# Transposing the row maxima in the bank of the next source, behind the values in even units, with a split low part and earlier statistics

## The chip, the cores and the metric

The kernel runs on one core of a Trainium2 chip. The metric is the device time of one execution in microseconds (us); lower is better. A core has a matmul engine (TensorE, PE in the profile, with its weight loads as PEld), a vector engine (VectorE, DVE), an activation engine (ScalarE, ACT), a general engine (GpSimd, POOL) and a queue engine that issues DMAs (SyncE, SP). Matmul results are written to PSUM, in banks of 128 partitions x 512 float32; VectorE and ScalarE read them there, GpSimd does not read PSUM in this kernel.

## The reference

One transformer block: self-attention with modulation, cross-attention on a context, and an MLP, for 16 samples of 256 tokens with width 256, 16 heads of width 16 and an MLP of 1024, in float32.

```python
x_norm = modulate(_ln(x), shift_a, scale_a)
q, k, v = jnp.split(x_norm @ W_qkv + b_qkv, 3, axis=-1)
attn_w = softmax(einsum('bhqd,bhkd->bhqk', q, k) * scale)
x = x + gate_a * (attn(attn_w, v) @ W_proj + b_proj)
q_c = _ln(x) @ W_qc + b_qc
k_c, v_c = jnp.split(_ln(context) @ W_kvc + b_kvc, 2, axis=-1)
x = x + cross_attn(q_c, k_c, v_c) @ W_cproj + b_cproj
x_norm2 = modulate(_ln(x), shift_m, scale_m)
x = x + gate_m * (gelu(x_norm2 @ W_mlp1 + b_mlp1) @ W_mlp2 + b_mlp2)
```

## The kernel before

**Units and beats.** The attention work is cut into 32 units, numbered from 0: a unit is the self-attention (s) or the cross-attention (c) of one sample. The order is s0 to s4, then s5, c0, s6, c1 and so on to s15, c10, then c11 to c15. So from unit 5 to unit 26 the odd units are s and the even ones c; from 26 on all are c. Each unit has eight beats, `beat(n, k)` with k from 0 to 7, and the code of a beat is the order in which each engine is given its work: PE, ACT, DVE, POOL and SP all keep program order, so an instruction that waits holds up everything behind it on its engine. After the units comes the MLP, which the change does not touch.

**What a beat holds.** A beat of unit n works on several units at once. `visit(n, k)` multiplies score rows of unit n + 1 into the bank pair s, whose row maxima VectorE then takes (TENSOR_REDUCE, mx<-s), and the transposed scores of unit n into the bank pair st. `exps()` then has ScalarE make the exponentials (pt<-st). Even beats add `av_part`, 16 matmuls of exponentials by values into a bank o (128*32 tiles). Odd beats add `lanes`, 24 projection matmuls in two interleaved chains for the queries, keys and values of units n + 2 and n + 3 and the output projection of an earlier unit. `cur`, `prev` and `nxt` are units n, n - 1 and n + 1; `q2`, `q3`, `q4` are units n + 2, n + 3, n + 4; `lc` is q4 and `lx` is q3 where they are cross-attentions, `ls` is q4 where it is a self-attention; `p1`, `p2`, `p3` are what follows the attention of units n - 1, n - 2, n - 3.

**Preparing a unit.** For unit n + 3 the layernorm has three steps: bn_stats (`steps[0]`), bn_aggr on VectorE with the power on GpSimd (`steps[1]`: mv, rs) and the normalised rows xn on GpSimd (`steps[2]`). TensorE transposes xn into a bank psT (`T.turn`, half f = 0 in beat 0 and f = 1 in beat 2 where the source is `ready`, both in beat 2 where not); ScalarE makes the high part of the result (`xTh`) and VectorE or GpSimd the low part (`xTl`), so that three matmuls of rounded numbers stand for one in float32. In the same way `to_stack` makes of the projected queries and keys a high part on ScalarE (`h_qc`, `h_k`) and a low part (`l_qc`, `l_k`): for each of two halves, f = 0 and 1, one VectorE instruction that reads the bank ps and subtracts the high part. DMAs on SP's queue carry both into the stack `big`, from which scores are multiplied.

**The maxima.** `m_part(u, half)` turns the maxima of half of a unit's heads: a transpose on TensorE (`psm`), a multiplication by -1 on ScalarE (`m`) and a DMA on SP into row 63 of the unit's queries, so that scores come out with the maximum subtracted. It stands in beat 0 (second half of unit n) and in beat 4 (first half of unit n + 1).

**Banks.** psm, psT and o come from two buffers in turn (`SHORT`), the projections from two others (`LONG`). A bank taken anew waits for the last reader of what it held: ps_k of beat 5 takes the bank of ps_qc, so it waits for the last reader of ps_qc; ps_qc of beat 1 takes that of ps_k or ps_kc. Sums of the exponentials come with o, are copied out by ScalarE (`oT`), fetched by a DMA as S (`pull`) and inverted (`recip`) in beat 2 of even units and beat 3 of odd ones.

Of the kernel before, what the change touches and what calls it, by code (L numbers as in the profile page):

```python
# [16 lines left out]
P = 128  # L17
# [4 lines left out]
def pixart_block(  # L22
# [45 lines left out]
    def ps_gen(name, tag=None):  # L68


        if tag is None and ps_turn[0] is not None:
            ps_turn[0] ^= 1
            tag = (SHORT, LONG)[ps_turn[0]]
        tag = tag or SHORT
        return psum.tile([P, 512], F32, tag=tag, name=name, bufs=2)
# [368 lines left out]
    def to_stack(W, src, bias, dst, which, name):  # L444

        o = Box()
        lo_row = (2, 1)[which]

        o.W, o.src, o.tok, o.name = W, src, False, name

        def first():
            o.ps = ps_gen(f"ps_{name}", LONG)
            mm3(o.ps[:, 0:N], W, 0, src.xT)

        def third():
            mm3(o.ps[:, N:], W, 1, src.xT)

        def second():  # L460
            third()
            high()

        def high():
            o.hi = work.tile([P, KC, N], F32R, tag="qkh", name=f"h_{name}", bufs=3)
            for f in range(KC):
                ACT.activation(o.hi[:, f], o.ps[:, f * N:(f + 1) * N], AF.Identity, bias=bias[f])

        def low():
            o.lo = work.tile([P, KC, N], F32R, tag="qkl", name=f"l_{name}", bufs=3)  # L470
            for f in range(KC):
                DVE.scalar_tensor_tensor(o.lo[:, f], o.ps[:, f * N:(f + 1) * N], bias[f], o.hi[:, f],
                                         ALU.add, ALU.subtract)

        def low_pool():
            o.lo = work.tile([P, KC, N], F32R, tag="qkl", name=f"l_{name}", bufs=3)
            y = work.tile([P, KC, N], F32, tag="y", name=f"y_{name}", bufs=1)
            for f in range(KC):
                ACT.activation(y[:, f], o.ps[:, f * N:(f + 1) * N], AF.Identity, bias=bias[f])
            POOL.tensor_tensor(o.lo, y, o.hi, ALU.subtract)  # L480

        def send(part, q=SP):

            row = (0, 3 - lo_row, lo_row)[part]
            q.dma_start(dst[row:row + 4 * 31 + 1:4].bitcast(F32), (o.hi if part < 2 else o.lo).bitcast(F32))

        o.send = send
        o.parts = [first, second, low]
        o.third = third
        o.low_pool = low_pool  # L490
        o.high, o.low = high, low
        o.send_high = lambda: [send(part) for part in range(2)]
        o.send_low = lambda: send(2)
        o.steps = [first, second]
        return o
# [169 lines left out]
                              AX.X, ALU.max)  # L665
        yield

    def m_part(u, hf):

        pst = ps_gen(f"psm_{u.n}_{hf}", SHORT)  # L670
        PE.transpose(pst[:16, :P], u.mx[:, hf].rearrange("p r a t -> p (r a t)"), ident)
        m = work.tile([16, P], F32R, tag="m", name=f"m_{u.n}_{hf}", bufs=1)
        ACT.mul(m, pst[:16, :P], -1.0)
        SP.dma_start(u.q[63:P:64, 4 * hf:4 * hf + 4, :].bitcast(F32), m.bitcast(F32))
# [309 lines left out]
    def beat(n, k):  # L984
# [24 lines left out]
                p2.end()  # L1009
        visit(n, k)  # L1010
        if k == 0:
            if cur:
                m_part(cur, 1)
            exps()
            if q3 and q3.ready:
                q3.T[0].place()
            if prev:
                av_part(prev, 3)
            if q3 and q3.ready:
                q3.T[0].turn((0,))  # L1020
            if q2:
                q2.K.low()
                q2.K.send_low()
# [16 lines left out]
        elif k == 2:  # L1040
            exps()
            if cur:
                av_part(cur, 0)
            if q3:
                q3.T[0].turn((1,) if q3.ready else (0, 1))
            if ls:
                ls.ln[0].steps[0]()
            elif prev:
                p1.recip()
                p1.spread()  # L1050
            if not (q3 and q3.kind == "c"):
                spare(n)
        elif k == 3:
            if q3:
                q3.T[0].high()
                if q3.kind == "c":
                    q3.T[0].full()
            exps()
            if alone and p2:
                p2.proj(0)  # L1060
                p2.proj(1)
            elif n:
                run(lanes(p2, q2 and q2.Q))
            else:
                run(lanes(q2.V, q2.Q))
            if q3 and q3.kind == "s":
                q3.T[0].low()
            if prev and ls:
                p1.recip()
                p1.spread()  # L1070
        elif k == 4:
            if nxt and lx:
                m_part(nxt, 0)
            exps()
            if nxt and not lx:
                m_part(nxt, 0)
            if alone:
                p2.end()
            if cur:
                av_part(cur, 1)  # L1080
            if lx:
                lx.T[1].turn()
            if q2:
                q2.Q.low()
                q2.Q.send_low()
            if q3 and q3.kind == "c":
                q3.T[0].rest_pool()
                spare(n)
            if ls:
                ls.ln[0].steps[1]()  # L1090
                ls.ln[0].steps[2]()
                ls.ready = True
        elif k == 5:
            exps()
            run(lanes(q3 and q3.K, (None if alone else p2) if n else q2.V))
            if cur:
                o_out(cur, 0)
            if lc:
                lc.ln[0].steps[1]()
                lc.ln[0].steps[2]()  # L1100
                lc.ready = True
            v = unit(n + 5)
            if v and v.kind == "c":
                load(v)
            if prev:
                p1.back()
        elif k == 6:
            exps()
            if lx:
                lx.T[1].high()  # L1110
            if cur:
                cur.post.begin()
                av_part(cur, 2)
                cur.post.pull(0)
            if q3 and p2:
                q3.vk = lanes(q3.V, q3.K)
                run(q3.vk, 1)
            if p3:
                p3.store()
            if lx:  # L1120
                lx.T[1].full()
                lx.T[1].rest_pool()
        elif k == 7:
            exps()
            run(q3.vk if q3 and p2 else lanes(q3 and q3.V, q3 and q3.K))
            if late:
                p2.add()
                p2.added = True
            elif lc:
                lc.ln[1].steps[0]()  # L1130
            v = unit(n + 5)
            if v and v.kind == "s":
                load(v)
            if n == nu - 1:
                p2.add()
                p2.store()
# [99 lines left out]
```

## Time and profile before

Three runs took 741.59, 742.77 and 743.25 us.

| | before |
|---|---|
| median of the runs | 742.77 us |
| profiled execution | 742.45 us |
| its span | 740.7 us |
| VectorE busy | 569.4 us (77%) |
| ScalarE busy | 556.1 us (75%) |
| GpSimd busy | 528.5 us (71%) |
| granted TensorE clock | 0.999 |

By stretches of the span (columns: busy us of each engine with its instructions, granted clock, share of the DMA engines, GB/s):

```profile
0.00:35.00 35.00, 31.43 (x230) 26.68 (x232) 20.96 (x49) 19.62 (x37) 23.68 (x33) 1.00 0.60 200
35.00:547.00 512.00, 503.44 (x7167) 385.63 (x7165) 417.07 (x636) 416.49 (x654) 386.68 (x385) 1.00 0.51 167
547.00:740.70 193.70, 187.33 (x1612) 186.04 (x1612) 131.38 (x198) 119.97 (x282) 118.18 (x108) 0.99 0.25 70
```

The units take the middle stretch; the columns are PE, PEld, DVE, ACT and POOL. A row of a timeline gives the start in us, the time in us from the first start to the last end of the group, engine, line, operation, result <- operands and the count; where an engine was idle ahead of it, brackets say how long and what released it. Most instructions are issued by one helper, so all have line 51 and are told apart by the names of their tiles. A row of waits has the waiting engine and tile, what it waited for, and in total us, times and longest us.

### The profile page before, as it was taken

How to read it: one execution, taken by the hardware profiler on the slowest of the kernel's cores; microseconds unless marked ns; L12 is line 12 of the kernel's file. 1: busy time of each engine (PE TensorE's matmuls, PEld its weight loads, DVE VectorE, ACT ScalarE, POOL GpSimd, SP SyncE). 2: the span in 40 equal slices, each digit the busy share in tenths (PEclk: the TensorE clock that was granted, in tenths of full speed). 3: DMA queues.
4: the chain of work that ended last, by engine and by line, in shares of the span. 5: the costliest groups of instructions: out<-in, count | busy, mean ns of one | idle time of the engine just before them, and what ended most of it. 6: DMA issues, size and time to landing. Idle time of an engine off the chain costs nothing.

```text
span 740.7 us, 22556 instructions
## 1 busy us (share of the span) xinstructions
PE 722.2 (98%) x9003; PEld 598.4 (81%) x9003; DVE 569.4 (77%) x882; ACT 556.1 (75%) x972; POOL 528.5 (71%) x525
## 2 busy tenths in 40 slices
PE   9999999999999999999999999999899999999997
PEld 8677777777777777777777787776479999999997
DVE  4778888878888887878788878778766877777762
ACT  5567888888888888887888888887766666666663
POOL 8465678797866868777686899985757676665663
PEclk9999999999999999999999999999999999999999
DMA  8365455544445455454555645545323132231311
GB/s 269 128 217 171 146 169 172 177 163 167 162 144 192 153 182 197 141 161 161 187 173 171 204 151 196 166 149 181 111 76 101 58 86 65 64 87 44 86 53 48
DMA packets 81388, 106.15 MB, mean 143 GB/s; under 512 B 16450, under 2 KB 44388, under 8 KB 81284
## 3 DMA queue, kind: packets, MB, share of 16 engines
q1 hardware_dynamic: 80180, 103.92, 43.3%
q8 instruction: 71, 1.16, 0.7%
q10 hardware_dynamic: 1104, 0.79, 0.4%
q14 instruction: 33, 0.27, 0.1%
HBM read 35.89 MB, written 8.98 MB: 61 GB/s over the span
## 4 chain that ended last, share of the span: by engine, by line
PE 92%; DVE 3%; ACT 2%; DMA 1%; issue 1%; POOL 1%; SPq 0%; ACTq 0%; POOLq 0%
PE s L51 18%; PE o L51 16%; PE st L51 14%; PE ph L51 13%; PE ps_P_s L51 4%; PE ps_k L51 3%; PE ps_v_s L51 3%; PE ps_kc L51 3%; PE ps_qc L51 3%; PE ps_v_c L51 2%; PE ps_q L51 2%; PE ps_P_c L51 2%; DVE mx L51 2%; PE psm L51 2%; PE psT_c L51 2%; PE psT_s L51 1%
## 5 line engine op out<-in xcount | busy, mean ns | idle before, releaser
L51 DVE TENSOR_REDUCE mx<-s 128x4 f32<-128x1024 f32 x252 | 307.7, 1221 | 89.2 <-PE s L51 88.7
L51 ACT ACTIVATE pt<-st 128x1024 f32<-128x1024 f32 x256 | 262.3, 1024 | 62.3 <-PE st L51 62.0
L51 PE MATMUL o<-pt,v 128*32 128x256 f32 x2048 | 137.1, 385 | 0.0
L51 PE MATMUL s<-big 63*128 63x256 f32 x1008 | 119.1, 307 | 5.5 <-DVE mx L51 4.0
L51 PE MATMUL st<-big 64*128 64x256 f32 (+1 forms) x1040 | 109.5, 284 | 3.1 <-ACT pt L51 1.7
L51 POOL TENSOR_TENSOR hl<-hf,hh 128x512 fp32r<-128x512 f32 x64 | 84.3, 1335 | 28.1 <-ACT hh L51 28.1
L51 PEld LDWEIGHTS s<-big 63*128 63x128 f32 x1008 | 79.0, 185 | 30.4 <-DVE mx L51 16.1
L51 PEld LDWEIGHTS st<-big 64*128 64x128 f32 (+1 forms) x1040 | 82.7, 186 | 6.6 <-ACT pt L51 3.4
L51 PEld LDWEIGHTS o<-pt,v 128*32 128x32 f32 x2048 | 53.4, 109 | 38.5
L51 ACT ACTIVATE hf<-ph,bT 128x256 f32<-128x256 f32 x120 | 50.4, 473 | 27.9 <-PE ph L51 27.9
L51 ACT ACTIVATE hh<-ph,bT 128x256 fp32r<-128x256 f32 x120 | 50.5, 472 | 20.9 <-PE st L51 9.8
L51 PE MATMUL ph<-wqch,wself 128*128 128x256 f32 x256 | 51.8, 286 | 1.3 <-ACT hh L51 1.3
L51 PE MATMUL ph<-wkch,wself 128*128 128x256 f32 x256 | 51.8, 286 | 0.0
L51 DVE TENSOR_SCALAR xn_m<-x,mv_m,rs_m 128x256 f32<-128x256 f32 x32 | 38.4, 1239 | 16.0 <-POOL rs_m L51 16.0
L51 PE MATMUL s<-big,hh 128*128 128x256 f32 x256 | 45.3, 276 | 0.0
L51 PE MATMUL st<-big,hh 128*128 128x256 f32 x256 | 45.0, 276 | 0.0
L51 PEld LDWEIGHTS ph<-wqch,wself 128*128 128x128 f32 x256 | 41.9, 191 | 1.9 <-ACT hh L51 1.5
L51 PEld LDWEIGHTS ph<-wkch,wself 128*128 128x128 f32 x256 | 41.9, 191 | 0.3
L51 POOL TENSOR_SCALAR xn_q<-x,mv_q,rs_q 128x256 f32<-128x256 f32 x32 | 38.9, 1225 | 1.7
L51 POOL TENSOR_SCALAR xn_c<-c,mv_c,rs_c 128x256 f32<-128x256 f32 x32 | 38.9, 1225 | 1.7
L51 PEld LDWEIGHTS s<-big,hh 128*128 128x128 f32 x256 | 38.8, 188 | 0.0
L51 PEld LDWEIGHTS st<-big,hh 128*128 128x128 f32 x256 | 38.8, 188 | 0.0
(214 smaller groups left out, 2215.7 us busy)
## 6 DMA issues: line engine op xcount, KB each, us to landing
big<-h_kc SPq DMA_DIRECT2D x32, 256.0 KB
big<-h_qc SPq DMA_DIRECT2D x32, 256.0 KB
big<-h_k SPq DMA_DIRECT2D x31, 256.0 KB
big<-h_q SPq DMA_DIRECT2D x31, 256.0 KB
big<-l_k SPq DMA_DIRECT2D x16, 256.0 KB
big<-l_q SPq DMA_DIRECT2D x16, 256.0 KB
g<-gd SPq DMA_DIRECT2D x16, 256.0 KB
U_s<-oT SPq DMA_DIRECT2D x32, 128.0 KB
```

The lines of the kernel that those rows point to most:

```text
L51: i = f(*a, **k)
```

## The change

Three places move.

1. **Beat 0.** `m_part` is split into `m_turn` (TensorE) and `m_row` (ScalarE and the DMA). Where unit n + 3 is `ready` at that point (units 1 to 28; "early"), the maxima are transposed into the second half of psT's bank and not a bank of their own, and the two transposes of psT for f = 0 come right behind, ahead of `av_part(prev, 3)` and not after it. ScalarE's exponentials now come ahead of `m`.
2. **Beat 4 of units where q3 is not a cross-attention.** `m_part(nxt, 0)` comes behind `av_part(cur, 1)`. Where q3 is a self-attention and n > 0 (units 1, 2, 4, ... 22; "half"), the low part of the queries is made by `low_first` (VectorE, f = 0) and `low_second` (f = 1: ScalarE writes y, GpSimd subtracts the high part), ahead of `m_part`, and is sent behind it.
3. **Statistics.** Where q4 is a cross-attention and q3 is not (units 2, 4, ... 22), bn_aggr and the power of q4's first layernorm move from beat 5 to the end of beat 2, on VectorE right behind the reciprocal.

```diff
+        def low_first():
+            o.lo = work.tile([P, KC, N], F32R, tag="qkl", name=f"l_{name}", bufs=3)
+            DVE.scalar_tensor_tensor(o.lo[:, 0], o.ps[:, :N], bias[0], o.hi[:, 0], ALU.add, ALU.subtract)
+
+        def low_second():
+            y = work.tile([P, KC, N], F32, tag="y", name=f"y_{name}", bufs=1)
+            ACT.activation(y[:, 1], o.ps[:, N:], AF.Identity, bias=bias[1])
+            POOL.tensor_tensor(o.lo[:, 1], y[:, 1], o.hi[:, 1], ALU.subtract)
...
-    def m_part(u, hf):
-
-        pst = ps_gen(f"psm_{u.n}_{hf}", SHORT)
+    def m_part(u, hf, pst=None):
+        m_row(u, hf, m_turn(u, hf, pst))
+
+    def m_turn(u, hf, pst=None):
+
+        if pst is None:
+            pst = ps_gen(f"psm_{u.n}_{hf}", SHORT)
         PE.transpose(pst[:16, :P], u.mx[:, hf].rearrange("p r a t -> p (r a t)"), ident)
+        return pst
+
+    def m_row(u, hf, pst):
+
         m = work.tile([16, P], F32R, tag="m", name=f"m_{u.n}_{hf}", bufs=1)
         ACT.mul(m, pst[:16, :P], -1.0)
...
         if k == 0:
-            if cur:
-                m_part(cur, 1)
+            early = q3 and q3.ready
+            if early:
+                q3.T[0].place()
+            pst = m_turn(cur, 1, q3.T[0].ps[:, N:] if early else None)
+            if early:
+                q3.T[0].turn((0,))
             exps()
-            if q3 and q3.ready:
-                q3.T[0].place()
+            m_row(cur, 1, pst)
             if prev:
                 av_part(prev, 3)
-            if q3 and q3.ready:
-                q3.T[0].turn((0,))
...
             if not (q3 and q3.kind == "c"):
                 spare(n)
+            if lc and not lx:
+                lc.ln[0].steps[1]()
...
             exps()
-            if nxt and not lx:
-                m_part(nxt, 0)
             if alone:
                 p2.end()
             if cur:
                 av_part(cur, 1)
+            half = q2 and q3 and q3.kind == "s" and n
+            if half:
+                q2.Q.low_first()
+                q2.Q.low_second()
+            if nxt and not lx:
+                m_part(nxt, 0)
+            if half:
+                q2.Q.send_low()
             if lx:
                 lx.T[1].turn()
-            if q2:
+            if q2 and not half:
                 q2.Q.low()
                 q2.Q.send_low()
...
             if lc:
-                lc.ln[0].steps[1]()
+                if lx:
+                    lc.ln[0].steps[1]()
                 lc.ln[0].steps[2]()
```

How instructions stand on the engines, in unit 8 (tile names carry running numbers). TensorE in beat 0, from the transpose of the maxima to the next score rows, before:

```order
L51 MATMUL psm_1_2973<-ident,mx_2643 16x128
L51 MATMUL o_2_2906<-pt_6_2899,v_79 32x256
L51 MATMUL o_2_2906<-pt_7_2934,v_79 32x256
...
L51 MATMUL psT_s_2980<-ident,xn_s_2843 128x128 [waits Activation_49,Pool_49]
L51 MATMUL psT_s_2980<-ident,xn_s_2843 128x128 [waits Pool_49]
L51 MATMUL s<-big_75 128x256 [waits DVE_49]
```

and now:

```order
L51 MATMUL psT_s_2974<-ident,mx_2645 16x128
L51 MATMUL psT_s_2974<-ident,xn_s_2844 128x128 [waits Pool_49] x2
L51 MATMUL o_2_2907<-pt_6_2900,v_79 32x256
L51 MATMUL o_2_2907<-pt_7_2935,v_79 32x256
...
L51 MATMUL s<-big_75 128x256 [waits DVE_49]
```

The maxima's transpose is written to psT's bank, the two transposes of xn follow it at once, and the o group is now the last ahead of s; psT waits for GpSimd's xn alone and no longer for ScalarE.

ScalarE in beats 4 and 5, from the high part of the queries on, before:

```order
L51 ACTIVATE h_qc_3115<-ps_qc_3012,bP 128x256
L51 ACTIVATE pt_4_3129<-st 128x1024 [waits PE_49,Activation_49]
L51 ACTIVATE m_0_3133<-psm_0_3131 16x128 [waits DMAHW3_49,PE_49,Activation_49]
L51 ACTIVATE pt_5_3157<-st 128x1024 [waits PE_49,Activation_49]
```

and now:

```order
L51 ACTIVATE h_qc_3121<-ps_qc_3012,bP 128x256
L51 ACTIVATE pt_4_3135<-st 128x1024 [waits PE_49,Activation_49]
L51 ACTIVATE y_qc_3147<-ps_qc_3012,bP 128x256 [waits DVE_49,Pool_49]
L51 ACTIVATE m_0_3152<-psm_0_3150 16x128 [waits DMAHW3_49,PE_49,Activation_49]
L51 ACTIVATE pt_5_3165<-st 128x1024 [waits PE_49]
```

y is new, reads the bank ps_qc as VectorE's half of the low part does, and waits for VectorE. TensorE's ps_k of beat 5, which takes that bank, changes what it waits for: `L51 MATMUL ps_k_3159<-xTh_s_3082,wself 128x256 [waits DVE_49]` becomes `L51 MATMUL ps_k_3167<-xTh_s_3088,wself 128x256 [waits Activation_49]`.

VectorE from beat 2 to beat 5, before:

```order
L51 RECIPROCAL S_s_2916<-S_s_2916 128x32 [waits DMAHW7_49,DMAHW5_49]
L51 TENSOR_REDUCE mx_2966<-s 128x2x2 [waits PE_49]
L51 SCALAR_TENSOR_TENSOR xTl_s_3083<-psT_s_2980,sc_97,xTh_s_3082 128x256 [waits Activation_49,Pool_49]
...
L51 SCALAR_TENSOR_TENSOR l_qc_3144<-ps_qc_3012,bP,h_qc_3115 128x256 [waits Activation_49]
L51 SCALAR_TENSOR_TENSOR l_qc_3144<-ps_qc_3012,bP,h_qc_3115 128x256
L51 TENSOR_REDUCE mx_2966<-s 128x2x2 [waits PE_49]
L51 BN_AGGR mv_c_3186<-st_c_3039 128x2 [waits DVE_49] x2
```

and now:

```order
L51 RECIPROCAL S_s_2917<-S_s_2917 128x32 [waits DMAHW7_49,DMAHW5_49]
L51 BN_AGGR mv_c_3073<-st_c_3039 128x2 [waits DVE_49] x2
L51 TENSOR_REDUCE mx_2967<-s 128x2x2 [waits PE_49]
L51 SCALAR_TENSOR_TENSOR xTl_s_3089<-psT_s_2974,sc_97,xTh_s_3088 128x256 [waits Activation_49,Pool_49]
...
L51 SCALAR_TENSOR_TENSOR l_qc_3145<-ps_qc_3012,bP,h_qc_3121 128x256 [waits Activation_49]
L51 TENSOR_REDUCE mx_2967<-s 128x2x2 [waits PE_49] x3
```

The two bn_aggr stand behind the reciprocal, which waits for DMAs, and ahead of the row maxima of beat 3; one of the two l_qc is gone.

1 line of the change is left out of this document (added).

## The prediction

> **What bounds the kernel now.** I read the page's table of engines first, then the shares of the chain of waits, then the waits by engine, and then the timeline of TensorE and VectorE around each place that the diff touches.
>
> ```profile
> span 740.7 us, 22556 instructions
> PE 722.2 (98%) x9003; PEld 598.4 (81%) x9003; DVE 569.4 (77%) x882; ACT 556.1 (75%) x972; POOL 528.5 (71%) x525
> PE 92%; DVE 3%; ACT 2%; DMA 1%; issue 1%; POOL 1%; SPq 0%; ACTq 0%; POOLq 0%
> PEld s L51 <- DVE mx L51: 16.1, 30, 1.3
> ```
>
> TensorE sets the time: 722.2 of 740.7 us, and 92% of the chain. Its longest list of waits is for VectorE's row maxima. So the change pays where TensorE pauses between groups of matmuls, and costs where it makes TensorE wait. The execution in the profile took 742.45 us, 1.75 us of it outside the span; the median of the runs is 742.77. Sums are made against 742.45 and carried over to the median.
>
> **Part 1: beat 0.** TensorE in beat 0 of unit 18 (even units are 6, 8, ... 26 with cross-attention; units are counted along the trace from 0), and VectorE beside it:
>
> ```profile
> 323.66 0.40 PE L51 MATMUL st<-big 64*128 64x256 f32 x4
> 323.99 0.28 PE L51 MATMUL psm<-ident,mx 128*16 128x128 f32 x1
> 324.19 1.07 PE L51 MATMUL o<-pt,v 128*32 128x256 f32 x16
> 325.20 0.44 PE L51 MATMUL psT_s<-ident,xn_s 128*128 128x128 f32 x2
> 325.56 0.50 PE L51 MATMUL s<-big 63*128 63x256 f32 x4
> 326.14 0.28 PE L51 MATMUL ps_qc<-xTh_q,wqch 64*128 64x256 f32 x1
> 325.01 0.86 DVE L51 SCALAR_TENSOR_TENSOR l_kc<-ps_kc,bP,h_kc 128x256 fp32r<-128x256 f32 x2
> ```
>
> From the start of psm to the next s it takes 325.56 - 323.99 = 1.57 us: 0.20 to the first o, 1.01 for the o group, 0.36 for the two psT (their distance is 0.165, so 0.20 more until s). The change puts psT between psm and o. The trace of before has no psm followed by psT; the nearest row is a psm followed by another matmul with a 128*128 tile:
>
> ```profile
> 35.24 0.28 PE L51 MATMUL psm<-ident,mx 128*16 128x128 f32 x1
> 35.36 0.96 PE L51 MATMUL cpm<-sT,wf 128*128 128x16 f32 x8
> ```
>
> It follows 0.12 us later, and not 0.20. So the new order is 0.12 to psT, 0.11 for its second matmul (eight cpm stand (0.96 - 0.28)/7 = 0.10 apart, the two psT now 0.165), 0.20 to o, as psm to o had, and 1.00 from o to s: 1.43, a saving of 0.14. Not all of it arrives. The matmuls of beat 1 (ps_qc, 326.14) take their bank from l_kc, which ends at 325.87. A matmul whose weight load waits for a semaphore loses more than the wait:
>
> ```profile
> 206.15 0.39 PE L51 MATMUL ps_k<-xTh_s,wself 64*128 64x256 f32 x1
> 206.38 0.28 PE L51 MATMUL ps_k<-xTh_s,wself 64*128 64x256 f32 x1
> 205.24 0.86 DVE L51 SCALAR_TENSOR_TENSOR l_qc<-ps_qc,bP,h_qc 128x256 fp32r<-128x256 f32 x2
> ```
>
> Here ps_k starts 0.05 after the l_qc that it waits for (205.24 + 0.86 = 206.10), and the next one 0.23 later and not 0.11 to 0.12. So beat 1 gets nothing for starting earlier than 325.87 + 0.05 + 0.11 = 326.03: **0.11 us a unit** at most. The early turn is made in units 1 to 28; I count it in 24, without the four of part 3, whose beat 3 waits for a DMA anyway. 24 x 0.107 = -2.6 us. Bounds: 0 (0.20 from psm to psT, as from psm to o, and 0.165 between the two as now: 1.57 again) and 24 x 0.14 = -3.4.
>
> The Trainium skill, TensorEngine Tiling (Array Packing), Key Properties, says that changing the tiling mode drains TensorE; psm is a 128*16 tile and psT 128*128, and by that rule the gain would be near 0. The row at 35.24 does not show such a drain, so I give the rule a chance and not the forecast.
>
> **Part 2: beats 4 and 5 of even units.** Unit 10, TensorE, then VectorE, then ScalarE:
>
> ```profile
> 202.21 0.28 PE L51 MATMUL ps_qc<-xTh_q,wqch 64*128 64x256 f32 x1
> 203.81 0.45 PE L51 MATMUL st<-big 64*128 64x256 f32 x4
> 204.33 0.27 PE L51 MATMUL psm<-ident,mx 128*16 128x128 f32 x1
> 204.53 1.07 PE L51 MATMUL o<-pt,v 128*32 128x256 f32 x16
> 205.53 0.50 PE L51 MATMUL s<-big 63*128 63x256 f32 x4
> 202.18 1.22 DVE L51 TENSOR_REDUCE mx<-s 128x4 f32<-128x1024 f32 x1 [0.38 <-PE s L51]
> 203.32 0.87 DVE L51 SCALAR_TENSOR_TENSOR xTl_s<-psT_s,sc,xTh_s 128x256 fp32r<-128x256 f32 x2
> 204.10 1.21 DVE L51 TENSOR_REDUCE mx<-s 128x4 f32<-128x1024 f32 x1
> 204.55 1.02 ACT L51 ACTIVATE pt<-st 128x1024 f32<-128x1024 f32 x1
> 205.46 0.25 ACT L51 ACTIVATE m<-psm 16x128 fp32r<-16x128 f32 x1
> ```
>
> psm starts 0.52 after the st group, and 0.33 in beat 0; 0.05 of that is the group's own 0.45 against 0.40, the other 0.14 is the wait for xTl_s (ends 204.19), whose bank psm takes. Behind av the wait is over, and s of beat 5 comes at 205.39 and not 205.53. But that is not what the next matmuls wait for. VectorE runs without a gap from the reduce at 202.18 through l_qc, and ps_k starts at 206.15 because l_qc ends at 206.10. In the change VectorE does one half of l_qc, the row below says 474 ns, and ScalarE writes the other half (y) first; the new order has ps_k wait for ScalarE, and y for VectorE, as both read one bank. What ScalarE needs for a half and to start after VectorE on one bank:
>
> ```profile
> L51 DVE SCALAR_TENSOR_TENSOR l_qc<-ps_qc,bP,h_qc 128x256 fp32r<-128x256 f32 x32 | 13.8, 474 | 0.0
> L51 ACT ACTIVATE hf<-ph,bT 128x256 f32<-128x256 f32 x120 | 50.4, 473 | 27.9 <-PE ph L51 27.9
> 560.74 1.00 DVE L51 TENSOR_SCALAR xTf_m<-psT_m,sc,cpT 128x256 f32<-128x256 f32 x2 [1.63 <-PE psT_m L51]
> 561.83 1.02 ACT L51 ACTIVATE wkch<-psT_m,cpT,sc 128x256 fp32r<-128x256 f32 x2 [0.75 <-DVE xTf_m L51]
> ```
>
> The hop is 561.83 - 561.74 = 0.09. So y starts at 205.24 + 0.47 + 0.09 = 205.80, ends at 206.28, and ps_k starts at 206.33: **0.18 us later than now**. Two halves one after the other on two engines, with two hops, are longer than two halves on one. It is in 12 units: 1, and 2, 4, ... 22. 11 x 0.175 and half of it for unit 1 (an estimate: its VectorE has more idle time) = +2.0 us. Bounds: y without the hop, 11 x 0.08 = +0.9; y free of VectorE, right behind pt where m starts now (205.46 + 0.47 + 0.05 = 205.98), 11 x -0.17 = -1.9. I take the wait, for the order of the change shows it and the trace has its like.
>
> The Trainium skill, PSUM — Partial Sum Buffer, section "PSUM bank collisions raise a hardware error", says that two engines that touch one bank in the same partitions are kept apart by a dependency, reads and other columns included. By that y cannot run beside VectorE's half, and the row at 561.83 agrees.
>
> Behind y on ScalarE stand m and pt of beat 5. pt would be ready when its st ends (206.13 by the earlier s) and gets ScalarE at 206.28 + 0.25 = 206.53 and not at 206.38 as now; it ends 207.55. Lanes and the s behind them hold TensorE from 202.21 to 203.81 a beat earlier, 1.60, so the next st comes at 206.33 + 1.60 = 207.93 and does not wait. The subtraction on GpSimd, the later row of maxima and the later store of the low part are needed only by score tiles and projections of later beats; the lanes, 24 matmuls a beat, lie between and cover them. Without that cover the row of maxima, which now stands behind pt in beat 0, would cost up to pt's 1.02 a unit.
>
> **Part 3: statistics in beat 2.** Two bn_aggr go behind the reciprocal and ahead of the next reduce.
>
> ```profile
> L51 DVE BATCH_NORM_AGGREGATE mv_c<-st_c 128x2 f32<-128x6 f32 x32 | 3.8, 160 | 0.0
> 233.93 0.35 DVE L51 RECIPROCAL S_s<-S_s 128x32 f32<-128x32 f32 x1 [0.62 <-DMA S_s<-oT]
> 234.20 1.16 DVE L51 TENSOR_REDUCE mx<-s 128x4 f32<-128x1024 f32 x1
> 330.45 0.35 DVE L51 RECIPROCAL S_s<-S_s 128x32 f32<-128x32 f32 x1 [1.23 <-DMA S_s<-oT]
> 330.72 1.16 DVE L51 TENSOR_REDUCE mx<-s 128x4 f32<-128x1024 f32 x1
> ```
>
> Two of them in a row take some 0.24 and delay what follows by 0.16, as they overlap with it. In unit 10 VectorE idles 0.38 ahead of the reduce, which hides it; so it is in seven of the eleven units (2 to 22, even). In units 12, 14, 16 and 18 (first and last quoted) the reciprocal waits for its DMA and the reduce follows at once, so that the whole chain of part 2 starts 0.16 later. The sums also leave later: in beat 0 o starts 0.43 after psm and not 0.20, so it ends 0.23 later; its copy on ScalarE now stands behind pt and some 0.11 of that is left (an estimate: ScalarE takes m and pt in turn). 4 x 0.27 = +1.1 us; bounds 0 and, with 0.32 for the pair and the full 0.23, 4 x 0.55 = +2.2.
>
> **Part 4: units 25 and 27.** There the statistics stay in beat 5, and psT needs the normalised rows a whole o group sooner.
>
> ```profile
> 434.82 2.43 POOL L51 TENSOR_SCALAR xn_c<-c,mv_c,rs_c 128x256 f32<-128x256 f32 x2
> 436.54 0.28 PE L51 MATMUL psm<-ident,mx 128*16 128x128 f32 x1
> 437.75 0.44 PE L51 MATMUL psT_c<-ident,xn_c 128*128 128x128 f32 x2
> 466.91 2.43 POOL L51 TENSOR_SCALAR xn_c<-c,mv_c,rs_c 128x256 f32<-128x256 f32 x2
> 468.77 0.28 PE L51 MATMUL psm<-ident,mx 128*16 128x128 f32 x1
> ```
>
> xn_c ends at 437.25 and 469.34. The second psT would start 0.23 after psm, 436.77 and 469.00; with a hop of 0.05 TensorE waits 0.53 and 0.39. That is 0.92; GpSimd's chain is set by VectorE and DMAs and may not follow the gain of the unit ahead, 0.1 more in part. I take +1.0 us; bounds 0.4 (xn_c follows by 0.25 in each) and 1.2.
>
> **Sum.** -2.6 + 2.0 + 1.1 + 1.0 = +1.5 us: 743.95 against the profiled 742.45, and **744.3 us** against the median.
>
> **Rivals.**
> 1. *Slower, a drain between psm and psT.* If the change from the 128*16 tile to 128*128 costs what psm to o costs, part 1 gives nothing and the rest stays: 742.77 + 4.1 = 746.9. It decides from 0.20 at that place on. For it: every other change of tile in beat 0 takes 0.20. Against: 35.36.
> 2. *Faster: ScalarE's y is early.* If y does not wait for VectorE's half, or VectorE reaches it sooner, part 2 gives -1.9 and not +2.0: 742.77 - 2.6 - 1.9 + 1.1 + 1.0 = 740.4. For it: ScalarE is free at 205.46. Against: the wait in the new order.
> 3. *No change: parts 3 and 4 are covered.* If the sums come in time and GpSimd's xn_c is ahead, -2.6 + 2.0 = -0.6: 742.2. For it: seven units have idle time there. Against: the rows of units 12 to 18.
>
> **How the numbers follow.** About 0.2% (1.5 us) is what a measurement of this kernel can tell from no change. Forecast 0.42, rival 1 0.16, rival 2 0.22, rival 3 0.20. The forecast's own range, 742.6 to 745.8, straddles that bound: 0.28 slower, 0.14 same. With rival 1 (0.16 slower), rival 2 (0.20 faster, 0.02 same), rival 3 (0.16 same, 0.02 on either side): faster 0.22, same 0.32, slower 0.46. The range goes from the middle of rival 2 to that of rival 1, 740.4 to 747.0, which leaves out half of each, some 0.2.
>
> **What would show it.** Right: psm to psT 0.12 and psm to s 1.43; beat 1's ps_qc about 0.1 after l_kc; y starting 0.09 after VectorE's half and ps_k 0.05 after y; TensorE waiting for xn_c in units 25 and 27; the reciprocals of units 12 to 18 followed at once by bn_aggr. Wrong: psT 0.20 after psm, y running beside l_qc, or VectorE idle ahead of the reduce in units 12 to 18.

## The result and the profile after

The changed kernel took 744.25 us (median of 20 runs, 742.02 to 747.87) against 743.31 us for the kernel before (20 runs, 740.66 to 749.95) on the same chips: a ratio of 1.0007, with a 95% interval of 0.9987 to 1.0027. Single runs of one kernel lie up to 9 us apart, so this is "no change that can be measured", with the middle 0.94 us on the slower side. Its profiled execution took 743.04 us, against 742.45.

From the page of the changed kernel: span, engines, and the shares of the chain that ended last.

```profile
span 741.1 us, 22513 instructions
PE 721.1 (97%) x9003; PEld 598.8 (81%) x9003; DVE 565.3 (76%) x870; ACT 563.8 (76%) x984; POOL 537.2 (72%) x537
PE 78%; DVE 8%; POOL 5%; DMA 3%; issue 3%; ACT 2%; SPq 0%; ACTq 0%; POOLq 0%; DVEq 0%
```

From its view of waits (total us, times, longest):

```profile
PEld s L51 <- DVE mx L51: 23.2, 51, 1.3
```

TensorE is busy 1.1 us less, and the span is 0.4 us longer: it waits more. Its share of the chain falls from 92% to 78%, and the wait for the row maxima grows from 16.1 to 23.2 us. The engines that gained work are ScalarE (+7.7 us) and GpSimd (+8.7); VectorE lost 4.1.

Beat 0 of unit 18 in the changed kernel, TensorE and then VectorE, as in the prediction's first timeline:

```profile
325.36 0.28 PE L51 MATMUL psT_s<-ident,mx 128*16 128x128 f32 x1
325.47 0.38 PE L51 MATMUL psT_s<-ident,xn_s 128*128 128x128 f32 x2
325.78 1.07 PE L51 MATMUL o<-pt,v 128*32 128x256 f32 x16
326.78 0.51 PE L51 MATMUL s<-big 63*128 63x256 f32 x4
327.36 0.31 PE L51 MATMUL ps_qc<-xTh_q,wqch 64*128 64x256 f32 x1
326.37 0.87 DVE L51 SCALAR_TENSOR_TENSOR l_kc<-ps_kc,bP,h_kc 128x256 fp32r<-128x256 f32 x2
```

The transpose of xn follows that of the maxima after 0.11 us, and from the one to the next s it is 326.78 - 325.36 = 1.42 us, where it was 1.57. ps_qc comes 0.12 after l_kc ends (327.24), so the rest of the gain is cut off there.

Beats 4 and 5 of the same unit, TensorE, VectorE, ScalarE:

```profile
332.94 0.44 PE L51 MATMUL st<-big 64*128 64x256 f32 x4
333.31 1.07 PE L51 MATMUL o<-pt,v 128*32 128x256 f32 x16
334.31 0.28 PE L51 MATMUL psm<-ident,mx 128*16 128x128 f32 x1
334.52 0.51 PE L51 MATMUL s<-big 63*128 63x256 f32 x4
335.45 0.38 PE L51 MATMUL ps_k<-xTh_s,wself 64*128 64x256 f32 x1 [0.19 <-ACT y_qc L51]
334.36 0.47 DVE L51 SCALAR_TENSOR_TENSOR l_qc<-ps_qc,bP,h_qc 128x256 fp32r<-128x256 f32 x1
334.92 0.47 ACT L51 ACTIVATE y_qc<-ps_qc,bP 128x256 f32<-128x256 f32 x1 [0.22 <-DVE l_qc L51]
```

VectorE's half ends at 334.83, y starts 0.09 later, and ps_k 0.06 after y ends. TensorE idles for it, and the row says for whom.

To compare traces, I take the start of the st group of each beat and the distance to the next one, and subtract the distance in the first trace of before. Summed over the units named, in us (a second trace of each of the two kernels comes from the experiments below):

| | before, again | after | after, again |
|---|---|---|---|
| beats 0 to 2, units 1 to 28 but 25 and 27 | +0.04 | -2.81 | -2.81 |
| beats 0 and 1, units 25 and 27 | -0.01 | +0.33 | +1.56 |
| beat 3, even units 2 to 22 | -0.01 | +1.27 | +1.23 |
| beats 4 and 5, even units 2 to 22 | +0.02 | +1.89 | +1.87 |
| beat 7, units 14 and 20 | 0.00 | +0.76 | +1.85 |
| odd units 3 to 23, beats 4 to 7 | 0.00 | -0.35 | -0.33 |
| up to the end of unit 0, and units 29 to 31 | +1.16 | -0.30 | +0.76 |

Beats 0, 4 and 5 come back to within 0.05 us in every unit. Beat 3, the ends of units 14 and 20, units 25 and 27 and the edges do not: they hang on DMAs or GpSimd. The -0.01 of beat 3 hides +0.57 in unit 2 and -0.61 in unit 18; unit 18 gives about as much back in nearly every later trace (0.45 to 0.61; 0.11 in one), so it is the first trace of before that is long there. Over all units, the second trace of before ends 1.31 us later than the first, the two of the changed kernel 0.88 and 4.00 later.

### The profile page after: what moved, and what is told of

It is laid out like the page before. It is cut to its first block, busy times and chain, and to the rows that moved or that the text cites. A ratio compares the mean times of both kernels' runs of the same rounds, so it can differ in the third digit from the quotient of the medians.

```text
span 741.1 us, 22513 instructions
## 1 busy us (share of the span) xinstructions
PE 721.1 (97%) x9003; PEld 598.8 (81%) x9003; DVE 565.3 (76%) x870; ACT 563.8 (76%) x984; POOL 537.2 (72%) x537
## 3 DMA queue, kind: packets, MB, share of 16 engines
q8 instruction: 71, 1.16, 0.7%
## 4 chain that ended last, share of the span: by engine, by line
PE 78%; DVE 8%; POOL 5%; DMA 3%; issue 3%; ACT 2%; SPq 0%; ACTq 0%; POOLq 0%; DVEq 0%
PE s L51 16%; PE ph L51 13%; PE st L51 12%; PE o L51 12%; DVE mx L51 5%; PE ps_P_s L51 3%; PE ps_k L51 3%; PE ps_q L51 3%; PE ps_kc L51 2%; PE ps_v_c L51 2%; PE ps_v_s L51 2%; PE ps_qc L51 2%; DMA S_s<-oT 2%; PE psT_c L51 1%; DVE xTl_s L51 1%
## 5 line engine op out<-in xcount | busy, mean ns | idle before, releaser
L51 DVE TENSOR_REDUCE mx<-s 128x4 f32<-128x1024 f32 x252 | 307.9, 1222 | 93.9 <-PE s L51 90.7
L51 ACT ACTIVATE pt<-st 128x1024 f32<-128x1024 f32 x256 | 262.6, 1026 | 47.3 <-PE st L51 44.3
L51 PE MATMUL o<-pt,v 128*32 128x256 f32 x2048 | 137.0, 385 | 0.0
L51 PE MATMUL s<-big 63*128 63x256 f32 x1008 | 119.2, 308 | 5.7 <-DVE mx L51 4.5
L51 PE MATMUL st<-big 64*128 64x256 f32 (+1 forms) x1040 | 109.1, 282 | 3.1 <-ACT pt L51 1.7
L51 PEld LDWEIGHTS s<-big 63*128 63x128 f32 x1008 | 78.5, 185 | 34.1 <-DVE mx L51 23.2
L51 POOL TENSOR_TENSOR hl<-hf,hh 128x512 fp32r<-128x512 f32 x64 | 83.8, 1326 | 28.7 <-ACT hh L51 28.7
L51 PEld LDWEIGHTS st<-big 64*128 64x128 f32 (+1 forms) x1040 | 82.7, 186 | 6.2 <-ACT pt L51 3.3
L51 PEld LDWEIGHTS o<-pt,v 128*32 128x32 f32 x2048 | 53.4, 109 | 39.7 <-issue 4.3
L51 ACT ACTIVATE hf<-ph,bT 128x256 f32<-128x256 f32 x120 | 50.4, 473 | 27.6 <-PE ph L51 27.6
L51 ACT ACTIVATE hh<-ph,bT 128x256 fp32r<-128x256 f32 x120 | 50.5, 472 | 21.4 <-PE s L51 10.7
L51 PE MATMUL ph<-wqch,wself 128*128 128x256 f32 x256 | 51.8, 286 | 1.3 <-ACT hh L51 1.3
L51 PE MATMUL ph<-wkch,wself 128*128 128x256 f32 x256 | 51.8, 286 | 0.0
L51 DVE TENSOR_SCALAR xn_m<-x,mv_m,rs_m 128x256 f32<-128x256 f32 x32 | 38.0, 1226 | 16.0 <-POOL rs_m L51 16.0
L51 PE MATMUL s<-big,hh 128*128 128x256 f32 x256 | 45.3, 276 | 0.0
L51 PE MATMUL st<-big,hh 128*128 128x256 f32 x256 | 45.0, 276 | 0.0
L51 POOL TENSOR_TENSOR U_s<-U_s,R_s 128x512 f32<-128x512 f32 x16 | 20.6, 1285 | 32.3 <-DMA R_s<-rd_s 18.5
L51 PEld LDWEIGHTS ph<-wqch,wself 128*128 128x128 f32 x256 | 41.9, 191 | 1.9 <-ACT hh L51 1.5
L51 PEld LDWEIGHTS ph<-wkch,wself 128*128 128x128 f32 x256 | 41.9, 191 | 0.3
L51 ACT COPY oT<-o 128x512 f32<-128x512 f32 x64 | 37.1, 579 | 5.4 <-PE o L51 3.0
L51 POOL TENSOR_SCALAR xn_q<-x,mv_q,rs_q 128x256 f32<-128x256 f32 x32 | 38.9, 1225 | 1.7
L51 PE MATMUL ps_k<-xTh_s,wself 64*128 64x256 f32 (+1 forms) x232 | 37.8, 288 | 2.2 <-ACT y_qc L51 2.0
```

What stands on the lines that cost most here:

```text
L51: i = f(*a, **k)
```

## The experiments

All were timed in five rounds beside the kernel before; ratios are to it, with 95% intervals. A kernel is called faster or slower where its interval leaves out 1. Each has one trace, of one of its runs.

**before_again and after_again.** No edit.

> The kernel of before once more, to see which stalls of a trace come back. If the late sums (the reciprocal of S waiting for its DMA) belong to the program, they stand again in units 12, 14, 16 and 18 with 0.6 to 1.2 us; if they belong to one execution, in other units or with other lengths. The lengths of beats 0, 4 and 5 should come back to within 0.05 us by either.

Measured: 743.78 us, 0.9991 (0.9968 to 1.0013). Beat 3 of unit 18, where the reciprocal waited 1.23 us for S in the first trace, is 0.61 shorter, and that of unit 2 0.57 longer; units 12, 14 and 16 came back with the same lengths, in unit 14 without the wait of 0.62.

> The changed kernel once more. The theory: beat 0 is 0.15 us shorter than before, beat 1 takes 0.04 back, beats 4 and 5 of even units 2 to 22 are 0.18 longer together, each to within 0.03, as in its first trace; the 0.3 to 0.7 that units 6, 10, 12 and 16 lost in beat 3 came from one long DMA issue on SP ahead of S in that execution and stands in other units or is gone. The rival: the loss belongs to the change (maxima's row behind the exponentials, statistics behind the reciprocal) and stands in the same units with the same size, some 1.8 us in all.

Measured: 745.88 us, 1.0017 (0.9996 to 1.0039). Beats 0, 4 and 5 as expected. Beat 3 lost 1.23 us again, but in units 2, 8, 10, 12 and 16 (0.50, 0.28, 0.28, 0.20, 0.53) and not in 6, 10, 12 and 16 (0.36, 0.47, 0.31, 0.67). Neither theory is met cleanly: three units repeat, with other sizes, and the total is the same (unit 18 gives 0.61 back in both).

**turn_alone: part 1 alone.** The changed kernel with these edits:

```diff
-            half = q2 and q3 and q3.kind == "s" and n
+            half = False
...
-            if lc and not lx:
-                lc.ln[0].steps[1]()
...
             exps()
+            if nxt and not lx:
+                m_part(nxt, 0)
...
-            if nxt and not lx:
-                m_part(nxt, 0)
...
-                if lx:
-                    lc.ln[0].steps[1]()
+                lc.ln[0].steps[1]()
```

> Part 1 of the change alone (beat 0: shared bank, early transposes, exponentials ahead of m); queries' low part, statistics and the place of psm in beat 4 as before. The theory: beats 0 and 1 give 0.107 us in each of units 1 to 24, 26 and 28 (26 x 0.107 = 2.8), units 25 and 27 lose 0.2 to 0.4 each waiting for xn_c, beats 4 and 5 are as before: 2.2 us faster, some 740.5 to 741.5. The rival: the later sums (o 0.23 later) take it back in even units, beat 3 longer by 0.1 to 0.3 there: no change.

Measured: 741.76 us, 0.9968 (0.9952 to 0.9983), faster. By beats: -2.82 us in the 26 units, +0.93 in units 25 and 27, beats 4 and 5 within 0.23, beat 3 of even units +0.66. The rival's 0.1 to 0.3 in all even units is not there, but five of them (2, 4, 6, 14, 20), where the reciprocal waited 0.7 to 1.2 us for the sums, lost 0.08 to 0.53.

**half_alone: part 2 alone.** Beat 0 and the statistics as before; of the diff stay `low_first`, `low_second` and in beat 4:

```diff
-            if nxt and not lx:
-                m_part(nxt, 0)
...
+            half = q2 and q3 and q3.kind == "s" and n
+            if half:
+                q2.Q.low_first()
+                q2.Q.low_second()
+            if nxt and not lx:
+                m_part(nxt, 0)
+            if half:
+                q2.Q.send_low()
```

> Part 2 alone (psm behind the values in beat 4, half of the queries' low part by ScalarE and GpSimd); beat 0 and the statistics as before. The theory: y waits for VectorE's half, ps_k for y, beats 4 and 5 together 0.18 longer in units 2, 4, ... 22: 2.0 us slower, some 745. The rival: the shorter beat 0 pushed the even units against VectorE in the full change, and alone the part costs nothing.

Measured: 744.95 us, 1.0022 (1.0004 to 1.0041), slower. Beats 4 and 5 cost +1.89 us in units 2 to 22, as in the full change. And unit 14 lost 1.49 us at its end; the timeline of TensorE and of SP's queue tells why, in half_alone:

```profile
277.58 0.50 PE L51 MATMUL s<-big 63*128 63x256 f32 x4 [1.30 <-DMA big<-l_qc]
271.80 0.54 SPq L51 DMA_DIRECT2D big<-l_qc  x1
```

and the same issue in before:

```profile
270.54 0.54 SPq L51 DMA_DIRECT2D big<-l_qc  x1
```

The scores of the next unit wait 1.30 us for the DMA of the queries' low part. It is issued 11.35 us after the unit's first st, and 10.87 in before: ScalarE's and GpSimd's steps come one after the other. These 0.48 us alone are not the cause, for unit 16 issues it at 11.78 and waits for nothing. In the trace's semaphore events this DMA lands in 16 parts: 15 of them 2.2 to 2.4 us after the issue in both units, the last one after 2.4 in unit 16 and after 5.5 in unit 14.

**stats_alone: part 3 alone.**

```diff
+            if lc and not lx:
+                lc.ln[0].steps[1]()
...
             if lc:
-                lc.ln[0].steps[1]()
+                if lx:
+                    lc.ln[0].steps[1]()
                 lc.ln[0].steps[2]()
```

> Part 3 alone: bn_aggr behind the reciprocal in beat 2 of even units. The theory: 0.16 longer in beat 3 only in units whose reciprocal waits for the sums' DMA, as in units 12, 14 and 16 of before, and nothing elsewhere: 0.3 to 1.0 us slower in all, which the runs cannot tell from no change, but the lengths of beats can. The rival: it costs 0.16 in all eleven units (1.8 us).

Measured: 744.22 us, 1.0014 (0.9989 to 1.0039), not told from no change. Beat 3 of even units 2 to 22 +0.43 in all: +0.44 in unit 2 and +0.67 in 16, -0.61 in 18, nothing above 0.04 in the others. The rival's 0.16 in all eleven is out. Unit 24, which the edit does not touch, lost 1.00: losses of this size come without it. What the pair costs in a late unit is worked out below, from all traces.

**move_alone: psm behind the values, nothing else.**

```diff
             exps()
-            if nxt and not lx:
-                m_part(nxt, 0)
...
             if cur:
                 av_part(cur, 1)
+            if nxt and not lx:
+                m_part(nxt, 0)
```

> The psm of beat 4 behind the values, nothing else. The theory: beat 4 of even units 0.14 shorter, beat 5 0.14 longer, since ps_k still waits for VectorE's low part at the same time: no change, 0 us within 0.3. The rival: half of it is kept, 0.07 x 12 = 0.8 us faster.

Measured: 743.28 us, 0.9990 (0.9964 to 1.0015). Beat 4 gave 1.49 us and beat 5 took 1.54: moving psm is worth nothing. Its beat 3 lost 1.37 us, as much as in the full change, though neither the statistics nor beat 0 differ from before.

**y_ahead: the full change, ScalarE's y ahead of the exponentials of beat 4** (`low_y` is the ScalarE half of `low_second`).

```diff
             q2.Q.high()
+            if q3 and q3.kind == "s" and n:
+                q2.Q.low_y()
             q2.Q.send_high()
```

> The full change with one ScalarE instruction moved: y of the second half right behind the high part, ahead of the exponentials of beat 4, so that it is done before VectorE's half begins. The theory (ps_k is late because y waits for VectorE's half on its bank): ps_k no longer waits for y; instead pt of beat 4 is 0.4 later and the next st waits for it, so that beats 4 and 5 together are about 0.05 longer than before and not 0.18: some 1.4 us under the changed kernel. The rival (y is slow for another reason, or splitting costs as such): 0.18 or more as in the changed kernel.

Measured: 742.50 us, 0.9986 (0.9965 to 1.0008). Unit 18, ScalarE, VectorE and TensorE:

```profile
331.78 0.47 ACT L51 ACTIVATE y_qc<-ps_qc,bP 128x256 f32<-128x256 f32 x1
332.14 1.03 ACT L51 ACTIVATE pt<-st 128x1024 f32<-128x1024 f32 x1
332.45 0.47 DVE L51 SCALAR_TENSOR_TENSOR l_qc<-ps_qc,bP,h_qc 128x256 fp32r<-128x256 f32 x1
333.22 0.50 PE L51 MATMUL st<-big 64*128 64x256 f32 x4
333.56 0.28 PE L51 MATMUL ps_k<-xTh_s,wself 64*128 64x256 f32 x1
```

y is over before VectorE's half, st now waits for the exponentials (333.22 - 333.17 = 0.05), and ps_k follows st without a pause. Beats 4 and 5 together cost -0.59 us over the eleven units where the changed kernel has +1.89: -0.05 a unit, expected +0.05. That mean mixes two kinds of unit: the seven whose beat 3 lost nothing have +0.06 on average, as expected, and units 6, 8, 12 and 20, which had lost 0.24 to 1.41 there, have -0.18 to -0.29. In these VectorE is late and has one half left to do where it had two; that this is the reason was not tried. With the wait of y for VectorE gone, the 0.17 a unit are gone: it is this wait that made part 2 dear.

**turn_but_two: part 1, the old order in units 25 and 27.**

```diff
-            early = q3 and q3.ready
+            early = q3 and q3.ready and n not in (25, 27)
...
+            if q3 and q3.ready and not early:
+                q3.T[0].place()
             if prev:
                 av_part(prev, 3)
+            if q3 and q3.ready and not early:
+                q3.T[0].turn((0,))
```

> Part 1 alone, but not in units 25 and 27, which keep the old beat 0. The theory: the other 26 units keep their 0.11 us (2.8), units 25 and 27 lose nothing (they lost 0.2 and 0.7 in turn_alone), and the later sums cost 0.3 to 1.0 in a few even units: 1.8 to 2.5 us faster than before, some 741 us, about 1 us under turn_alone. The rival: GpSimd's xn_c is late in their neighbours 24, 26 or 28 instead, and it is no faster than turn_alone.

Measured: 742.96 us, 0.9998 (0.9971 to 1.0026): a miss. The 26 units gave -2.90, but units 25 and 27 lost 0.37 each, beat 3 +1.58 and the last unit +1.1 (it has +1.36 in the second trace of before, too). The first was the edit's own; unit 25, TensorE and ScalarE:

```profile
436.95 0.41 PE L51 MATMUL psT_c<-ident,xn_c 128*128 128x128 f32 x2 [0.33 <-ACT m L51]
436.56 0.25 ACT L51 ACTIVATE m<-psm 16x128 fp32r<-16x128 f32 x1
```

With psm in a bank of its own, psT takes that bank next and waits for m, which part 1 has put behind the exponentials. So sharing the bank is what makes that order of ScalarE free.

**sums_first: before, with S and U ahead of the keys' low part on SP's queue.** The same edit makes after_sums_first of the changed kernel.

```diff
                 q2.K.low()
-                q2.K.send_low()
+                if not prev:
+                    q2.K.send_low()
...
                 p1.pull(1)
+                if q2:
+                    q2.K.send_low()
```

> The kernel of before with one move on SP's queue: the DMA of the sums S (and of U) is issued ahead of the keys' low part l_k and not behind it. The theory: the reciprocal waits in some even units of every execution, other units each time, because S is issued only 3.4 us into the unit behind m and l_k, with 0.2 to 0.5 us to spare, and any slow DMA issue or landing uses that up; issued 0.6 sooner, the wait for S goes from 2 to 7 us in a trace to under 1, and the 0.6 to 2.5 us that beat 3 loses go with it: 0.5 to 2 us faster than before. The rival: what is slow is the landing of S, whatever its place, and nothing changes.

Measured: 741.41 us, 0.9974 (0.9959 to 0.9990), faster. The waits of the reciprocal for S fall from 3.2 us (six times) to 1.7 (twice) in the trace, less than expected: beat 3 lost nothing in most units and 0.70 in one, unit 8. SP and VectorE there:

```profile
169.09 0.60 SPq L51 DMA_DIRECT2D S_s<-oT  x1
173.24 0.35 DVE L51 RECIPROCAL S_s<-S_s 128x32 f32<-128x32 f32 x1 [1.32 <-DMA S_s<-oT]
```

S is issued in time and lands 4.1 us later, where it takes 1.8 in most units. So sums are late in two ways: issued late, behind a long issue on SP, which the move helps against, or slow to land, as the rival has it, which it does not. Where the runs gained is not shown: this trace is of the slowest of the twelve (745.15), its units start 2.24 us later than in before, and beat 3 of the even units has -0.03 in all.

> The changed kernel with the same move. The theory: its losses in beat 3 (1.3 us in each of its two traces) go, those of units 25 and 27, of beats 4 and 5 (0.18 x 11) and of units 14 and 20 (the scores of the next unit wait for the queries' low part) stay: about 1 to 1.5 us under the changed kernel, level with before. The rival: the two bn_aggr behind the reciprocal keep beat 3 late by 0.16 in eleven units.

Measured: 743.59 us, 1.0006 (0.9981 to 1.0031). Beat 3 lost +1.93 us in this trace, in units 2, 12 and 20 (1.01, 0.69, 0.84): against the expectation, the move did not rid the changed kernel of late sums. In all three S was issued 2.8 to 3.0 us after the unit's first st and landed 3.8 to 4.1 us after its issue, by its semaphore's events. The others have 0.03 or less each, so the rival's 0.16 in eleven units is out again.

**turn_sums_first: part 1, the old order in units 25 and 27 with m ahead of the exponentials there, and S and U ahead.** Beside the edits of turn_but_two and sums_first:

```diff
+            if not early:
+                m_row(cur, 1, pst)
             exps()
-            m_row(cur, 1, pst)
+            if early:
+                m_row(cur, 1, pst)
```

> Part 1 of the change with the old beat 0 in units 25 and 27, there with m ahead of the exponentials again (in turn_but_two psT waited for it), and the sums ahead of l_k; low part and statistics as before. The theory: 0.11 in each of 26 units (2.8), nothing lost in units 25 and 27, and the 0.6 to 2.5 us of late sums won too: 3.5 to 4.5 us faster than before, some 739 to 740. The rival: with the sums in time, beat 1's wait for l_kc takes more back, and it is no better than turn_alone (0.997 of before).

Measured: **739.07 us, 0.9947 (0.9923 to 0.9972)**, the fastest. From its page:

```profile
span 737.3 us, 22546 instructions
PE 90%; DVE 3%; POOL 3%; DMA 2%; ACT 2%; issue 1%; ACTq 0%; SPq 0%; POOLq 0%
```

and SP's queue in its unit 10:

```profile
197.42 0.58 SPq L51 DMA_DIRECT2D big<-m  x1
198.09 0.60 SPq L51 DMA_DIRECT2D S_s<-oT  x1
198.75 0.53 SPq L51 DMA_DIRECT2D U_s<-oT  x1
199.40 0.57 SPq L51 DMA_DIRECT2D big<-l_kc  x1
```

Beats 0 to 2 gave -3.02 us in the 26 units, units 25 and 27 0.00, beat 3 -0.05 (+0.53 in unit 12, where S landed 3.9 us after its issue, and -0.58 in unit 18). The interval overlaps that of turn_alone, so the runs do not tell how much the move of the sums adds to part 1.

**low_sent_late: before, with the queries' low part sent behind R.**

```diff
                 q2.Q.low()
-                q2.Q.send_low()
+                if not (q3 and q3.kind == "s" and n):
+                    q2.Q.send_low()
...
                 p1.back()
+            if q2 and q3 and q3.kind == "s" and n:
+                q2.Q.send_low()
```

> The kernel of before with one move on SP's queue: in units 1 and 2, 4, ... 22 the DMA of the queries' low part is issued behind the one of R, 0.65 us later; who computes it and when is as before. The theory: what units 14 and 20 lost at their end in every kernel with the split low part (0.3 to 1.5 us in one or both) is this DMA landing after the next unit's scores want it; sent 0.65 later without the split, the scores wait for l_qc in units 14 or 20 too, 0.5 to 1.5 us in all, and nothing else changes. The rival: the stall comes from the split itself (GpSimd, ScalarE); then the lengths of all beats are those of before.

Measured: 763.56 us, 1.0277 (1.0246 to 1.0308). The direction is as expected, the size is not: not two units but every one of the twelve loses 0.8 to 2.6 us about its end. The scores wait for that DMA in the view of waits:

```profile
PE s L51 <- DMA big<-l_qc: 12.4, 10, 2.5
PE s L51 <- DMA big<-l_q: 5.5, 3, 2.2
```

The rival, the split itself, is out as the only cause: here nothing is split. But the DMA also lands later. Unit 14, which lost 1.21 us at its end, has it issued 0.74 later than in before; SP and TensorE, in low_sent_late:

```profile
284.91 0.65 SPq L51 DMA_DIRECT2D R_s<-rd_s  x1
285.65 0.57 SPq L51 DMA_DIRECT2D big<-l_qc  x1
290.69 0.47 PE L51 MATMUL s<-big 63*128 63x256 f32 x3 [1.03 <-DMA big<-l_qc]
```

and in before, where l_qc is issued at 270.54:

```profile
271.18 0.65 SPq L51 DMA_DIRECT2D R_s<-rd_s  x1
275.13 0.48 PE L51 MATMUL s<-big 63*128 63x256 f32 x4
```

The semaphore events have its last part land 2.73 us after the issue in before, 1.86 ahead of these scores, and 4.90 after it in low_sent_late, behind R, which is as large (256 KB). Over the even units 2 to 22 the last part lands 2.3 to 4.4 us after the issue in before and 4.7 to 6.1 behind R. So the low part has room in before, 1.1 to 2.3 us in nine of these units and 0.24 and 0.37 in units 6 and 20, and what uses it up here is more the place behind R than the 0.74.

## Why the prediction was right

The time was forecast at 744.3 us and came out at 744.25. That these agree to 0.05 is luck: the forecast was +1.5 us on a kernel of 742.77, and the runs have +0.94 on one of 743.31, with an interval of about -1.0 to +2.0 that holds no change at all as well. Slower was given 0.46 and no change, which it was, 0.32. The traces can judge the terms, by the table above:

**Part 1, right in size, not in the count.** -2.6 us was forecast and -2.8 measured, in both traces and in turn_alone. The gain of a unit is as worked out, 0.107 forecast and 0.108 measured: 0.148 gross (-3.85 in beat 0), of which l_kc takes some back (+1.06 to +1.38 in beat 1). But units 12, 14, 16 and 18, which the forecast left out, gained like the others (0.09 to 0.16 each). The rival of a drain is out: psT comes 0.11 after psm. The Trainium skill, TensorEngine Tiling (Array Packing), Key Properties, says that changing the tiling mode drains TensorE; no drain shows at this change of tile, and whether the two tiles are two modes no run here shows. The change from psT to o in the same beat still takes 0.20 (the second psT starts at about 325.58, the first o at 325.78).

**Part 2, right.** 0.175 a unit, +2.0 with unit 1, was forecast; +1.89 was measured in the eleven even units, 0.172 each, and y_ahead shows that the wait of y for VectorE is its cause. The hop is the 0.09 read from another place. The Trainium skill, PSUM — Partial Sum Buffer, "PSUM bank collisions raise a hardware error", says that two engines that touch one bank in the same partitions are kept apart by a dependency, reads included; y's row, 0.09 behind VectorE's half, agrees. Unit 1 gave 0.15 in place of a small loss, and the odd units gave 0.35 that I had not worked out; about half of it stands in half_alone, and its cause was not looked for.

**Part 3, the total right by chance.** +1.1 us was forecast and +1.27 and +1.23 measured. But the step "in units 12, 14, 16 and 18 the reciprocal waits for its DMA" took one execution's stalls for the program's. Unit 10 of the changed kernel, VectorE and SP's queue:

```profile
201.97 0.35 DVE L51 RECIPROCAL S_s<-S_s 128x32 f32<-128x32 f32 x1 [0.97 <-DMA S_s<-oT]
202.24 0.19 DVE L51 BATCH_NORM_AGGREGATE mv_c<-st_c 128x2 f32<-128x6 f32 x2
202.34 1.19 DVE L51 TENSOR_REDUCE mx<-s 128x4 f32<-128x1024 f32 x1
196.32 2.29 SPq L51 DMA_DIRECT2D big<-h_kc  x2
200.01 0.60 SPq L51 DMA_DIRECT2D S_s<-oT  x1
```

Of its 0.47 us only 0.10 (202.24 to 202.34), and 0.03 by which the reduce takes longer than behind a reciprocal alone (1.19 against 1.16), is the pair of bn_aggr. The rest is S: the two issues of h_kc held SP for 2.29 us (1.51 in before, 1.21 in most units), and all DMAs behind them came later. turn_but_two (+1.58) and move_alone (+1.37), without the statistics, lose as much in beat 3, and half_alone (+0.24) less.

All traces together settle what the pair costs. I take each even unit from 2 to 22 whose beat 3 lost over 0.05 us to a wait for the sums (units 16 and 18 against their lengths without the 0.09 and 0.61 that they lose in the first trace of before), and subtract the loss from the reciprocal's wait. In 27 such cases without the pair this leaves 0.62 to 0.66 us, in 18 cases with it 0.49 to 0.53. So the first 0.64 us of a wait cost nothing, and the pair costs 0.13 in a late unit, where 0.16 was forecast, and nothing in the others. The mechanism stands, then, but not the list of units: which sums are late is the execution's. In units 14 and 18 of the changed kernel VectorE stands idle ahead of the reduce (0.23 and 0.46 us), which the prediction named as a sign of being wrong; unit 18:

```profile
331.30 1.22 DVE L51 TENSOR_REDUCE mx<-s 128x4 f32<-128x1024 f32 x1 [0.46 <-PE s L51]
```

Of the +1.27, some 0.5 is the pair in units 6, 10, 12 and 16; the rest is late sums, less the 0.61 that unit 18 did not lose again. The term for sums that leave later, 0.11 a unit, is not seen: where no issue ahead of it is long, S is issued 3.38 us after the unit's first st in both kernels. Part 1 takes room from it in another way, since the reciprocal that does not wait now comes 5.37 us after that st and not 5.5.

**Part 4, the wait right, its size not one number.** +1.0 us was forecast, with bounds of 0.4 and 1.2; +0.33 and +1.56 were measured, both outside them, +0.93 in turn_alone, and 0.00 in turn_sums_first, where these two units keep the old order. Unit 25 of after_again, TensorE and GpSimd:

```profile
438.80 0.33 PE L51 MATMUL psT_c<-ident,xn_c 128*128 128x128 f32 x1 [0.40 <-POOL xn_c L51]
436.31 2.44 POOL L51 TENSOR_SCALAR xn_c<-c,mv_c,rs_c 128x256 f32<-128x256 f32 x2
```

xn_c ends at 438.75 and psT follows. How long TensorE waits depends on how far GpSimd is behind in that execution.

**What was priced at nothing and was not.** The step "the later store of the low part ... the lanes cover them" failed. Units 14 and 20 lost 0.76 and 1.85 us together in the changed kernel, 1.49 in half_alone, 1.36 in y_ahead and 0.64 in after_sums_first. In the seven further traces without the split, low_sent_late aside, these two lost 0.53 in one and 0.01 or less in six. I looked at matmuls as the cover and not at how long the DMA takes to land. The changed kernel and half_alone issue it 0.4 to 0.5 us later where the unit has no other delay (11.22 to 11.35 us after the first st against 10.87). That is covered as long as all its parts land some 2.4 us after the issue; in units 14 and 20, where scores waited, the last part took 4.3 to 5.5. In sums_first it took 4.8 in unit 20 and cost 0.53 without the split. So of the 1.30 us in half_alone at most 0.48 is the later issue, if the landing moves with it (an estimate from these rows); the rest is that part, and what holds it is not known. In the first trace this loss, the odd units' gain and the edges of the program nearly cancel; in the second, whose units end 4.00 us later than before, they do not.

The rival of a faster kernel fell with part 2, that of covered terms with part 4. For part 3 the latter was right wherever the sums came in time; by its time alone, -0.6 us, the runs do not tell it from the forecast.

## What to carry to other kernels

Splitting the readers of one bank over two engines did not make them parallel here: they ran one after the other, plus a hop. Of the two orders tried, the split cost next to nothing in the one where the first half was done before the other engine arrived (y_ahead). A stall behind a DMA in one trace is not a property of its unit: take a second trace of the same kernel before pricing an edit by it, and compare the wait with the idle time that was there anyway. And the order of issues on one queue counts: small sums ahead of a large transfer gave 0.3% in the runs, one store moved behind another of its size cost 2.8%.

## What the runs showed of the hardware that was not expected

A matmul with a 128*16 tile followed by one with 128*128 starts 0.11 us later, as if the tile had not changed, while 128*128 to 128*32 takes 0.20. The issue of a DMA on SP's queue, 0.6 us as a rule, now and then takes 1 to 2 us, at other places in each kernel (h_kc of unit 10: 1.51 for two in before, 2.29 in after). And single transfers land late: S (8 KB) as a rule 1.8 to 2.0 us after its issue, but up to 4.1 (unit 8 of sums_first), and one of the 16 parts of l_qc after 5.5 us where the others take 2.2 to 2.4 (unit 14 of half_alone). What holds them was not tried.
